# Query and key columns inside the value products of a four-layer graph network, with a different order of the softmax and of the layers around it

## The chip, the cores and the metric

The kernel runs on one core of one Trainium2 chip. The metric is the device time of one execution in microseconds (us), median of several runs. A profiled execution gives the times of single instructions; its span is close to, but not the same as, the timed runs.

Engines are named as in the profile: PE (TensorE, matmul) with PEld (its weight loads), DVE (VectorE), ACT (ScalarE), POOL (GpSimd) and SP (SyncE, which here issues the DMAs). Matmuls write to PSUM, from which DVE and ACT read.

## The reference

128 graphs of 128 nodes with 512 features, and one weighted adjacency matrix each, go through four layers. Each layer's output is added to its input and normalized over the features. All data is float32.

```python
def reference(x, adj, ...):
    # layer 0: normalized adjacency (with self loops), times x, times a weight
    #   Ah = A + I;  dh = rsqrt(sum(Ah));  An = dh Ah dh;  out = relu(An x W0 + b0)
    x = layernorm(x + L0(x, adj))
    # layer 1: attention-like weights, one number per node
    #   q, k = split(x Wqk^T)  (64 columns each);  v = x Wv^T
    #   w = sum over m of (q k^T / 8) * adj;   w = softmax over the nodes;  out = w * v
    x = layernorm(x + L1(x, adj))
    # layer 2: mean over neighbours, joined with x
    #   agg = (A x) / deg;  out = relu([x, agg] W2^T)
    x = layernorm(x + L2(x, adj))
    # layer 3: like layer 0 without relu:  out = An (x W3 + b3)
    x = layernorm(x + L3(x, adj))
```

## The kernel before

**Tiling.** The graphs are taken in groups of four (`G = 4`, 32 groups, index `t`). One group's x is a tile of 128 partitions (nodes) by 4 x 512.

**Block products.** Each 512 x 512 weight is split into 2 x 2 blocks of 256, and a product of activations and weight is made of seven block products instead of eight (a Strassen-Winograd form), named B11, T1, B21, T2, B22, T3, T4 in `project` (L517). The activations are split the same way, over pairs of graphs (`q`), the two graphs of a pair (`r`) and the halves of the features (`h`). `left_sums` (L495) forms four sums of activation blocks on POOL (each 128 x 512 for a group), `weight_sums` (L373) the ones of the weights, once. One block product is four matmuls of 256 columns, each of which the profile shows as two instructions. The results meet in a few PSUM banks (`ps_b`, five of them); DVE and ACT read them out between the products into blocks `s`, `u2`, `u5`. `fin` adds a finished block to x; `norm_stats` (L613) and `norm_last` (L592) normalize rows.

**Layer 1.** `l1_turn` (L669) gives x transposed; `l1_qk` (L678) makes queries and keys by 16 matmuls of 128 columns per group into `p_qk`; ACT copies them out (`kd`, `qs`). `l1_scores` (L697) multiplies the adjacency by the keys (`p_sc`, 65 columns: 64 keys and one column that yields row sums `rs` for layer 3's bias) and reduces on DVE to one number `w` per node. `l1_softmax` (L717) turns `w` on PE (`p_w`) and forms the softmax `e`; `l1_weights` (L732) turns it back (`p_ws`) to `ws`. `l1_out` (L739) is the product of the values, where `fin` adds block times `ws` to x; parts that come before `ws` is known wait in a list.

**Aggregates.** `aggregate` (L458) multiplies x by an adjacency on PE into `p_agg` (`ps_t`, three banks), ACT copies it out. The adjacency of group t+1 is loaded, scaled and transposed in `prep` (L854: `load`, `prep_rows`, `prep_turn`); two hops through DRAM and DVE transposes do the turn. `turn_x` (L467) does the same with x for layers 1 and 2 (`xT1`, `xT2`): SP issues the copies to DRAM and back, DVE transposes 32 x 32 blocks.

**Order.** Every instruction is first recorded. PE's order is the one written out by hand in the loop below; `hooks` insert work behind a block product, and `tails` postpone the last product (T4) of a projection into the next one. A planner (`Plan.schedule`) then orders the other engines by due times which it derives from estimated durations. DVE, ACT, POOL and SP run their queues in that order.

The loop over groups works on group t in layers 0 and 1 and on group u = t-1 in layers 2 and 3:

```python
        if t > 1:
            l0_out(t, {B21: [lambda: l2_agg(u, 1)]})
            prep(t + 1)
            tails.append(lambda: l1_turn(t))
        l2_out(u, {T3: [lambda: l1_qk(t, 0)]} if t > 1 else {...})
        if t < last:
            l0_agg(t + 1)
        finish_tails()
        if t > 1:
            l1_qk(t, 1)
        l1_out(t, {B11: [lambda: l1_scores(t)], B21: [lambda: l1_softmax(t)], T3: [lambda: l3_agg(u)]})
        l3_bias(u)
        l3_out(u)
        if t < last:
            l2_turn(t)
            l2_agg(t, 0)
```

In the profile every instruction has the line of the planner's `emit` (L270), so groups are told apart by tile names.

Of the kernel before, what the change touches and what calls it, by code (L numbers as in the profile page):

```python
# [15 lines left out]
P = 128  # L16
# [6 lines left out]
ATT = 64  # L23
LN_EPS = 1e-5
# [286 lines left out]
def kernel(  # L311
# [32 lines left out]
    def load(t):  # L344
        if t == 1:
            a = tp.tile([P, 2, G, P], FP, tag="y", name="adj_1", bufs=3)[:, 0]
        else:
            a = ap.tile([P, G, P], FP, tag="adj", name=f"adj_{t}", bufs=1)
        nc.sync.dma_start(a, adj[t * G:(t + 1) * G].rearrange("g n m -> n g m"))
        xi = xp.tile([P, G, F], FP, tag="x", name=f"x_{t}")  # L350
        for g in range(0, G, 2 if t == 0 else G):
            k = slice(g, g + (2 if t == 0 else G))
            nc.sync.dma_start(xi[:, k], x[t * G:(t + 1) * G][k].rearrange("g n f -> n g f"))
        st["adj", t], st["x", t] = a, xi
# [38 lines left out]
    wqk_sb = const.tile([P, C, 2 * ATT], FP, tag="wqk_sb", name="wqk_sb")  # L393
    for b in range(Q):
        nc.sync.dma_start(wqk_sb[b * K:(b + 1) * K], wqkT.rearrange("(b c k) m -> b k c m", b=Q, c=C)[b])
    wv_sb = weight(wvT, "wv_sb", nc.sync, turned=True)
# [9 lines left out]
    def prep_rows(t):  # L406
        a = st["adj", t]
        deg = sp.tile([P, G], FP, tag="deg", name=f"deg_{t}")
        nc.vector.tensor_reduce(deg, a, AX.X, ALU.add)
        dh = sp.tile([P, G], FP, tag="dh", name=f"dh_{t}")  # L410
        nc.vector.tensor_scalar(dh, deg, 1.0, None, ALU.add)
        d = sp.tile([P, G], FP, tag="d", name=f"d_{t}")
        nc.gpsimd.tensor_tensor(d, dh, nhalf, ALU.pow)
        dm = sp.tile([P, G], FP, tag="dm", name=f"dm_{t}")
        nc.vector.tensor_scalar(dm, deg, DEG_EPS, None, ALU.max)
        rdeg = sp.tile([P, G], FP, tag="rdeg", name=f"rdeg_{t}")
        nc.vector.reciprocal(rdeg, dm)
        ana = tp.tile([P, 2, G, P], FP, tag="y", name=f"ana_{t}", bufs=3)
        nc.vector.tensor_tensor(ana[:, 0], a, ident[:, None, :].to_broadcast([P, G, P]), ALU.add)
        nc.vector.tensor_tensor(ana[:, 0], ana[:, 0], per_graph(d), ALU.mult)  # L420
        nc.vector.tensor_tensor(ana[:, 1], a, per_graph(rdeg), ALU.mult)
        st["ana", t], st["d", t], st["dm", t] = ana, d, dm
# [72 lines left out]
    def left_sums(name, t, eng=nc.gpsimd, pairs=(slice(0, 2),)):  # L495

        a = st[name, t].rearrange("p (q r) (h c) n -> p q r h c n", r=2, h=2)
        s = [tp.tile([P, 2, 2, P], FP, tag=f"s{i}", name=f"{name}s{i}_{t}", bufs=3) for i in (1, 2, 3, 4)]
        for q in pairs:
            a11, a12, a21, a22 = a[:, q, 0, 0], a[:, q, 0, 1], a[:, q, 1, 0], a[:, q, 1, 1]  # L500
            s1, s2, s3, s4 = (v[:, q] for v in s)
            eng.tensor_tensor(s1, a21, a22, ALU.add)
            eng.tensor_tensor(s2, s1, a11, ALU.subtract)
            eng.tensor_tensor(s3, a11, a21, ALU.subtract)
            eng.tensor_tensor(s4, a12, s2, ALU.subtract)
        st[name, t] = {B11: a[:, :, 0, 0], B21: a[:, :, 0, 1], B22: s[3], T4: a[:, :, 1, 1], T1: s[0], T2: s[1], T3: s[2]}
# [10 lines left out]
    def project(name, t, parts, first, c11, fin, hooks=None, after=lambda: None, early=True,  # L517
                when=lambda f: f(), pairs=(0, 1)):
# [26 lines left out]
        def block(tag):  # L545
            return tp.tile([P, 2, H], FP, tag=tag, name=f"{tag}_{name}_{t}", bufs=1 if tag in ("u5", "sb") else 2)[:, qs]
# [5 lines left out]
        if early:  # L552
            product(g, B21, False)
            when(lambda: c11(g, block))
# [4 lines left out]
        if not early:  # L559
            product(g, B21, False)  # L560
            when(lambda: c11(g, block))
# [6 lines left out]
        when(lambda: (fin(0, 1, u2), norm_stats(name, t, 0, pairs)))  # L568
# [100 lines left out]
    def l1_turn(t, turn=turn_x, rows=(0, 1)):  # L669
        if rows[0] == 0:  # L670
            left("xT1", t)
        for r in rows:
            turn("xT1", t, r)
        st["x1T", t] = st["xT1", t]
        if rows[-1] == 1:
            left_sums("xT1", t)

    def l1_qk(t, r):  # L678

        xT = st["x1T", t]  # L680
        if r == 0:
            st["p_qk", t] = ps_t.tile([P, G, 2 * ATT], FP, tag="pt", name=f"p_qk_{t}")
        p = st["p_qk", t]
        with nc.unit():
            for g in (r, 2 + r):
                for c in range(C):
                    nc.tensor.matmul(p[:, g, :], xT[:, g, c, :], wqk_sb[:, c, :], start=(c == 0), stop=(c == C - 1))
        if r == 0:
            return
        kd = tp.tile([P, G, ATT + 1], FP, tag="kd", name=f"kd_{t}", bufs=1)  # L690
        nc.scalar.copy(kd[:, :, 0:ATT], p[:, :, ATT:2 * ATT])
        nc.scalar.copy(kd[:, :, ATT], st["d", t])
        qs = tp.tile([P, G, ATT], FP, tag="qs", name=f"qs_{t}", bufs=1)
        nc.scalar.mul(qs, p[:, :, 0:ATT], 1.0 / ATT ** 0.5)
        st["qk", t] = qs, kd

    def l1_scores(t):  # L697


        qs, kd = st.pop(("qk", t))  # L700
        d, dm = st["d", t], st["dm", t]
        p = ps_t.tile([P, G, ATT + 1], FP, tag="pt", name=f"p_sc_{t}")
        with nc.unit():
            for g in range(G):
                nc.tensor.matmul(p[:, g, :], st["arT", t][:, g, :], kd[:, g, :], start=True, stop=True)
        w = sp.tile([P, G], FP, tag="w", name=f"w_{t}")
        scr = tp.tile([P, F], FP, tag="row", name=f"scr_{t}", bufs=1)[:, 0:G * ATT].rearrange("p (g a) -> p g a", g=G)
        nc.vector.tensor_tensor(scr, p[:, :, 0:ATT], qs, ALU.mult)
        nc.vector.tensor_reduce(w, scr, AX.X, ALU.add)
        nc.vector.tensor_tensor(w, w, dm, ALU.mult)  # L710
        rs = sp.tile([P, G], FP, tag="rs", name=f"rs_{t}")
        nc.vector.tensor_tensor(rs, p[:, :, ATT], dm, ALU.mult)
        nc.vector.tensor_tensor(rs, rs, d, ALU.add)
        nc.vector.tensor_tensor(rs, rs, d, ALU.mult)
        st["w", t], st["rs", t] = w, rs
# [16 lines left out]
    def l1_weights(t):  # L732
# [4 lines left out]
        st["ws", t] = ws  # L737

    def l1_out(t, hooks=None):  # L739
        z = st["x", t]  # L740

        def fin(r, h, blk):
            for q in range(2):
                g = 2 * q + r
                zg = z[:, g, h * H:(h + 1) * H]
                nc.vector.scalar_tensor_tensor(zg, blk[:, q, :], st["ws", t][:, g:g + 1], zg, ALU.mult, ALU.add)

        def when(f):
            if ("ws", t) in st:
                f()  # L750
            else:
                pending.append(f)

        def weights():
            l1_weights(t)
            for f in pending:
                f()

        pending = []
        hooks[T3] = [weights] + hooks[T3]  # L760
        project("v", t, [("xT1", wv_sb)], copy_first, lambda p, b: fin(0, 0, p), fin, hooks,
                early=False, when=when)
# [34 lines left out]
    def l3_agg(t):  # L797
        left("agg3", t)
        for g in (0, 2, 1, 3):
            aggregate("agg3", t, g, st["anT", t])  # L800
# [14 lines left out]
    def l3_out(t, left="agg3", pairs=(0, 1)):  # L815
        def fin(r, h, blk):
# [3 lines left out]
        project("o3", t, [(left, w3_sb)], copy_first, lambda p, b: fin(0, 0, p), fin,  # L820
                after=lambda: store(t), pairs=pairs)
# [9 lines left out]
    def begin():  # L831
# [7 lines left out]
        weight_sums(wv_sb, nc.vector)  # L839
        l0_out(1)  # L840
        l1_turn(0, turn_on_tensor, (0,))
        finish_tails()
        l1_qk(0, 0)
        l1_turn(0, turn_on_tensor, (1,))
        l1_qk(0, 1)
        for w in (w2x_sb, w2a_sb, w3_sb):
            weight_sums(w, nc.gpsimd)
        l1_out(0, {B11: [lambda: l1_scores(0)], B21: [lambda: l1_softmax(0)],
                   T3: [lambda: l1_turn(1, turn_on_tensor), lambda: l1_qk(1, 0)]})
        finish_tails()  # L850
        l1_qk(1, 1)
        l2_both(0, 0)

# [7 lines left out]
    for t in range(1, NT):  # L861
        u = t - 1
        if t > 1:
            l0_out(t, {B21: [lambda: l2_agg(u, 1)]})
            prep(t + 1)
            tails.append(lambda: l1_turn(t))
        l2_out(u, {T3: [lambda: l1_qk(t, 0)]} if t > 1 else {B21: [lambda: l2_both(0, 1), lambda: prep(2)]})
        if t < last:
            l0_agg(t + 1)
        finish_tails()  # L870
        if t > 1:
            l1_qk(t, 1)
        l1_out(t, {B11: [lambda: l1_scores(t)], B21: [lambda: l1_softmax(t)], T3: [lambda: l3_agg(u)]})
        l3_bias(u)
        l3_out(u)
        if t < last:
            l2_turn(t)
            l2_agg(t, 0)
# [5 lines left out]
    for q in range(2):  # L884
        l3_agg_pair(last, q, nc.gpsimd)
        l3_bias(last, (2 * q, 2 * q + 1))
        l3_out(last, f"agg3{q}", (q,))
# [33 lines left out]
```

## Time and profile before

| what | value |
|---|---|
| timed runs (3) | 2481.28 us median, 2480.01 to 2484.1 |
| profiled span | 2479.5 us, granted PE clock 0.998 |
| PE busy | 2458.4 us |
| DVE busy | 1813.6 us |
| POOL busy | 1336.5 us |
| ACT busy | 976.6 us |
| DMA | 241.24 MB in all, 97 GB/s mean |

A group of the profile is a set of like instructions: engine, operation, output tile and inputs, shape, count, busy time and mean length. The timeline of an engine gives start and length of its instructions in us from the span's start; an arrow in brackets names the idle time before one and what ended it. Since matmuls overlap in PE's pipeline, what one costs is read from the distance between starts.

### The profile page before, as it was taken

How to read it: one execution, taken by the hardware profiler on the slowest of the kernel's cores; microseconds unless marked ns; L12 is line 12 of the kernel's file. 1: busy time of each engine (PE TensorE's matmuls, PEld its weight loads, DVE VectorE, ACT ScalarE, POOL GpSimd, SP SyncE). 2: the span in 40 equal slices, each digit the busy share in tenths (PEclk: the TensorE clock that was granted, in tenths of full speed). 3: DMA queues.
4: the chain of work that ended last, by engine and by line, in shares of the span. 5: the costliest groups of instructions: out<-in, count | busy, mean ns of one | idle time of the engine just before them, and what ended most of it. 6: DMA issues, size and time to landing. Idle time of an engine off the chain costs nothing.

```text
span 2479.5 us, 37052 instructions
## 1 busy us (share of the span) xinstructions
PE 2458.4 (99%) x13486; PEld 2206.8 (89%) x13486; DVE 1813.6 (73%) x3165; ACT 976.6 (39%) x1989; POOL 1336.5 (54%) x1522
## 2 busy tenths in 40 slices
PE   8999999999999999999999999999999999999998
PEld 7898998989989889889899998998998999989987
DVE  7677777777777777777777777777777777777665
ACT  3334334443334344344433343433434334443335
POOL 6455555646455555555555564645555555655443
PEclk9999999999999999999999999999999999999999
DMA  5142434423434324344333343343442434433220
GB/s 178 35 111 74 106 93 113 121 82 88 108 97 124 100 75 115 89 116 112 81 97 102 103 124 94 77 107 93 124 111 69 110 90 115 118 80 88 77 60 34
DMA packets 392629, 241.24 MB, mean 97 GB/s; under 512 B 140288, under 2 KB 356864, under 8 KB 392448
## 3 DMA queue, kind: packets, MB, share of 16 engines
q1 hardware_dynamic: 392448, 238.88, 36.1%
q8 instruction: 107, 1.75, 0.3%
q14 instruction: 74, 0.61, 0.1%
HBM read 126.62 MB, written 112.20 MB: 96 GB/s over the span
## 4 chain that ended last, share of the span: by engine, by line
PE 98%; DMA 1%; ACT 0%; DVE 0%; SPq 0%; POOL 0%; issue 0%; ACTq 0%; POOLq 0%; DVEq 0%
PE p_o L270 62%; PE p_v L270 16%; PE p_agg L270 14%; PE p_qk L270 5%; PE p_sc L270 1%; DMA x<-in_x_dram 0%; SPq L270 0%; DVE x L270 0%; PE p_ws L270 0%; DMA w2x_sb<-in_L_gnn_W_dram 0%; PE p_w L270 0%; ACT xT L270 0%; PE p_xT L270 0%; POOL last L270 0%; ACT agg L270 0%
## 5 line engine op out<-in xcount | busy, mean ns | idle before, releaser
L270 ACT COPY agg<-p_agg 128x512 f32<-128x512 f32 x384 | 221.0, 583 | 578.6 <-PE p_agg L270 578.6
L270 PE MATMUL p_o<-w_sb,agg 128*128 128x256 f32 x1536 | 353.5, 379 | 1.2 <-ACT s_o L270 0.7
L270 PEld LDWEIGHTS p_o<-w_sb,agg 128*128 128x128 f32 x1536 | 286.6, 190 | 38.3 <-ACT s_o L270 1.1
L270 PE MATMUL p_o<-w2x_sb,xT2s 128*128 128x256 f32 x1024 | 263.0, 379 | 1.5 <-DVE xT2s L270 1.5
L270 PE MATMUL p_o<-w2a_sb,agg2s 128*128 128x256 f32 x1024 | 262.8, 379 | 0.0
L270 POOL TENSOR_TENSOR xT1s<-xT 128x512 f32<-128x512 f32 x64 | 94.3, 1473 | 286.7 <-DVE xT L270 228.8
L270 PE MATMUL p_agg<-anT,x 128*128 128x128 f32 x2048 | 243.9, 277 | 0.2 <-DVE anT L270 0.2
L270 PEld LDWEIGHTS p_agg<-anT,x 128*128 128x128 f32 x2048 | 235.5, 192 | 1.2 <-DVE anT L270 0.4
L270 PE MATMUL p_v<-wv_sb,xT1s 128*128 128x256 f32 x1024 | 233.3, 381 | 0.0
L270 PE MATMUL p_o<-w_sb,agg0s 128*128 128x256 f32 x1024 | 229.5, 382 | 3.5 <-DVE u_o L270 2.6
L270 POOL TENSOR_TENSOR agg3s<-agg 128x512 f32<-128x512 f32 x62 | 84.1, 1356 | 270.9 <-ACT agg L270 270.9
L270 PEld LDWEIGHTS p_o<-w_sb,agg0s 128*128 128x128 f32 x1024 | 192.6, 191 | 30.7 <-DVE u_o L270 3.0
L270 PEld LDWEIGHTS p_o<-w2x_sb,xT2s 128*128 128x128 f32 x1024 | 194.4, 190 | 28.3 <-DVE xT2s L270 2.0
L270 PE MATMUL p_o<-w_sb,agg3s 128*128 128x256 f32 x992 | 219.2, 379 | 0.0
L270 PEld LDWEIGHTS p_o<-w2a_sb,agg2s 128*128 128x128 f32 x1024 | 194.6, 190 | 26.5
L270 PEld LDWEIGHTS p_v<-wv_sb,xT1s 128*128 128x128 f32 x1024 | 189.6, 190 | 27.3
L270 PEld LDWEIGHTS p_o<-w_sb,agg3s 128*128 128x128 f32 x992 | 188.5, 190 | 25.6
L270 ACT ACTIVATE x<-x,nmro,rstdo 128x512 f32<-128x512 f32 x257 | 198.8, 809 | 4.3
L270 PE MATMUL p_o<-w2x_sb,xT 128*128 128x256 f32 x768 | 197.6, 380 | 1.8 <-ACT s_o L270 1.1
L270 PE MATMUL p_o<-w2a_sb,agg 128*128 128x256 f32 x768 | 197.1, 379 | 0.0
L270 DVE TENSOR_TENSOR u_o<-p_o,s_o 128x512 f32<-128x512 f32 (+1 forms) x132 | 89.2, 675 | 146.1 <-PE p_o L270 146.1
L270 PE MATMUL p_v<-wv_sb,xT 128*128 128x256 f32 x768 | 182.0, 380 | 1.9 <-DVE u_v L270 1.9
(141 smaller groups left out, 4674.8 us busy)
## 6 DMA issues: line engine op xcount, KB each, us to landing
x<-in_x_dram SPq DMA_DIRECT2D x31, 1024.0 KB, 5.1
out_dram<-x SPq DMA_DIRECT2D x31, 1024.0 KB, 5.4
xT2s<-x SPq DMA_DIRECT2D x120, 256.0 KB, 2.6
xT2y<-xT2s SPq DMA_DIRECT2D x240, 128.0 KB, 2.9
xT1s<-x SPq DMA_DIRECT2D x120, 256.0 KB, 2.5
xT1y<-xT1s SPq DMA_DIRECT2D x240, 128.0 KB, 3.3
sa<-ana SPq DMA_DIRECT2D x120, 128.0 KB, 3.4
ya<-sa SPq DMA_DIRECT2D x120, 128.0 KB, 3.2
```

Source lines behind the costliest of these rows:

```text
L270: getattr(getattr(self.nc, op.engine), method)(*[v.real() if isinstance(v, Ref) else v for v in args], **{k: v.real() if isinstance(v, Ref ...
```

## The change

- `l1_qk` goes. Queries and keys are 64 more columns of each weight block of the values (`V = H + ATT = 320`): the left column block gets the queries, the right one the keys, and the seven block products of `l1_out` compute them too. The result stays in SBUF in four tiles `v00` to `v11`; each pair q of a region has a PSUM bank of its own.
- Scores come behind the whole product of the values and layer 3's aggregates; `l1_softmax` is a hook of the first block product of `l3_out`, and `l1_add` (turn of the softmax, addition of `ws` times v to x, statistics) a hook of its third. `l3_out` takes B21 behind T1 (`early` false) except in the last group.
- Both halves of layer 2's aggregates move into the next `l0_out` (hooks B21 and T1); one half stood ahead of it before.
- The adjacency is loaded straight into the tile `ana` (tag `y`, three buffers) and scaled in place; the single buffer `adj` goes. The third sum of `left_sums` overwrites a block of its operand, so one of four tags of sums goes; `u2` has one buffer instead of two.
- The order of the first groups is written out anew: both `l1_out` products come before layer 2 of group 0, and the loop starts at t = 2.

```diff
-    wqk_sb = const.tile([P, C, 2 * ATT], FP, tag="wqk_sb", name="wqk_sb")
+    wqk_sb = tp.tile([P, C, 2 * ATT], FP, tag="row", name="wqk_sb", bufs=1)
 ...
-    wv_sb = weight(wvT, "wv_sb", nc.sync, turned=True)
+    wv_sb = const.tile([P, 2, 7, V], FP, tag="wv_sb", name="wv_sb")
+    for h in range(2):
+        for j in range(2):
+            for b in range(Q):
+                nc.sync.dma_start(wv_sb[b * K:(b + 1) * K, :, 2 * h + j, 0:H], ...)
+            nc.scalar.copy(wv_sb[:, :, 2 * h + j, H:V], wqk_sb[:, 2 * h:2 * h + 2, j * ATT:(j + 1) * ATT])
 ...
-            eng.tensor_tensor(s3, a11, a21, ALU.subtract)
+            eng.tensor_tensor(a21, a11, a21, ALU.subtract)
 ...
     def l1_scores(t):
-                nc.tensor.matmul(p[:, g, :], st["arT", t][:, g, :], kd[:, g, :], start=True, stop=True)
+                nc.tensor.matmul(p[:, g, :], st["arT", t][:, g, :], st["v", t][g % 2, 1][:, g // 2, H:V + 1],
+                                 start=True, stop=True)
-        nc.vector.tensor_tensor(scr, p[:, :, 0:ATT], qs, ALU.mult)
+        for r in range(2):
+            nc.vector.tensor_tensor(scr...[:, :, r], p...[:, :, r, 0:ATT], st["v", t][r, 0][:, :, H:V], ALU.mult)
         nc.vector.tensor_reduce(w, scr, AX.X, ALU.add)
-        nc.vector.tensor_tensor(w, w, dm, ALU.mult)
+        nc.vector.scalar_tensor_tensor(w, w, 1.0 / ATT ** 0.5, dm, ALU.mult, ALU.mult)
 ...
+    def l1_out(t, hooks):
+        def product(p, k, fresh, then):
+            for q in range(2):
+                with nc.unit():
+                    for c in range(2):
+                        nc.tensor.matmul(p[q], a[k][:, q, c, :], wv_sb[:, c, k, :], ...)
+                then(p[q], q)
+            for f in hooks.get(k, ()):
+                f()
+        def add(to, other):
+            return lambda p, q: nc.vector.tensor_tensor(to[:, q, 0:V], p, other[:, q, 0:V], ALU.add)
+        g = region()
+        product(g, B11, True, lambda p, q: nc.scalar.copy(s[:, q, 0:V], p))
+        finish_tails()
+        q5 = region()
+        product(q5, T1, True, add(out[1, 1], s))
+        product(g, B21, False, lambda p, q: nc.scalar.copy(out[0, 0][:, q, 0:V], p))
+        v = region()
+        product(v, T2, True, add(out[0, 1], s))
+        product(q5, B22, False, add(out[0, 1], out[0, 1]))
+        product(v, T3, False, add(out[1, 1], out[1, 1]))
+        product(v, T4, False, add(s, s))
+    def l1_add(t):
+        nc.tensor.transpose(p[:, :G], st.pop(("e", t)), ident[:G, :G])
+        nc.vector.tensor_copy(ws, p[:, :G])
+        for r in range(2):
+            for g in (r, 2 + r):
+                for h in range(2):
+                    nc.vector.scalar_tensor_tensor(zg, st["v", t][r, h][:, g // 2, 0:H], ws[:, g:g + 1], zg,
+                                                   ALU.mult, ALU.add)
+            norm_stats("v", t, r, (0, 1))
 ...
     def l3_agg(t):
-        for g in (0, 2, 1, 3):
+        for g in (0, 1, 3, 2):
 ...
     def begin():
+        l1_out(0, {T3: [lambda: l1_turn(1, turn_on_tensor)]})
+        l1_out(1, {B11: [lambda: l1_scores(0)], T1: [lambda: l1_softmax(0)], B21: [lambda: l1_add(0)]})
         l2_both(0, 0)
+        l2_out(0, {B21: [lambda: l2_both(0, 1), lambda: prep(2)], T2: [lambda: l1_scores(1)],
+                   B22: [lambda: l1_softmax(1)], T3: [lambda: l1_add(1)]})
+        l0_agg(2)
+        l2_turn(1)
+        l0_out(2, {B21: [lambda: l2_agg(1, 0)], T1: [lambda: l2_agg(1, 1)]})
+        l3_agg(0)
+        l3_bias(0)
+        l3_out(0)
 ...
-    for t in range(1, NT):
+    for t in range(2, NT):
         u = t - 1
+        if t > 2:
+            l0_out(t, {B21: [lambda: l2_agg(u, 0)], T1: [lambda: l2_agg(u, 1)]})
+        tails.append(lambda: l1_turn(t))
+        prep(t + 1)
+        l2_out(u)
         if t < last:
             l0_agg(t + 1)
-        l1_out(t, {B11: [lambda: l1_scores(t)], B21: [lambda: l1_softmax(t)], T3: [lambda: l3_agg(u)]})
+        l1_out(t, {})
+        l3_agg(u)
+        l1_scores(t)
         l3_bias(u)
-        l3_out(u)
+        l3_out(u, {B11: [lambda: l1_softmax(t)], B21: [lambda: l1_add(t)]})
         if t < last:
             l2_turn(t)
-            l2_agg(t, 0)
```

## The prediction

> **What bounds the kernel now.** I read the page first: busy time, then the chain that ended last.
>
> ```profile
> PE 2458.4 (99%) x13486; PEld 2206.8 (89%) x13486; DVE 1813.6 (73%) x3165; ACT 976.6 (39%) x1989; POOL 1336.5 (54%) x1522
> ...
> PE 98%; DMA 1%; ACT 0%; DVE 0%; SPq 0%; POOL 0%; issue 0%; ACTq 0%; POOLq 0%; DVEq 0%
> ```
>
> TensorE (PE) holds 98% of the chain. The list of PE's waits adds up to some 13 us, all near the start and the end; one period, from one block product of layer 2 to the same one of the next group, is 76.13 us (1045.66 to 1121.79) without a wait. So a PE instruction saved is time saved, and a PE wait added is time added. Next, PE in order of time in one group (start, length, instructions):
>
> ```profile
> 1016.11 1.95 PE L270 MATMUL p_qk<-wqk_sb,xT 128*128 128x128 f32 x16
> 1017.90 3.78 PE L270 MATMUL p_agg<-anT,x 128*128 128x128 f32 x32
> ...
> 1026.76 1.89 PE L270 MATMUL p_v<-wv_sb,xT 128*128 128x256 f32 x8
> 1028.49 1.00 PE L270 MATMUL p_sc<-kd,arT 128*128 128x65 f32 x8
> 1029.33 1.94 PE L270 MATMUL p_v<-wv_sb,xT1s 128*128 128x256 f32 x8
> 1031.11 1.89 PE L270 MATMUL p_v<-wv_sb,xT 128*128 128x256 f32 x8
> 1032.83 0.27 PE L270 MATMUL p_w<-ident,w 128*4 128x128 f32 x1
> ```
>
> Prices are differences of starts: sixteen instructions of 128 columns take 1.79 us (112 ns each), eight of 256 take 1.73 (216 ns), the eight of the scores 0.84. Two block products (3.5 us) lie between the scores and `p_w`, which turns their row sums `w`; until `p_ws` at 1038.22, which turns the softmax, three more (5.2 us). VectorE (DVE) and GpSimd (POOL) meanwhile:
>
> ```profile
> 1029.60 0.42 DVE L270 TENSOR_TENSOR scr<-p_sc,qs 128x256 f32<-128x256 f32 x1 [1.29 <-PE p_sc L270]
> 1030.05 0.42 DVE L270 TENSOR_REDUCE w<-scr 128x4 f32<-128x256 f32 x1
> 1030.51 1.24 DVE L270 TENSOR_TENSOR w<-w,dm 128x4 f32<-128x4 f32 x1
> ...
> 1033.60 0.27 DVE L270 TENSOR_REDUCE mx<-p_w 4x1 f32<-4x128 f32 x1
> ...
> 1034.56 0.15 DVE L270 RECIPROCAL rsum<-ssum 4x1 f32<-4x1 f32 x1 [0.43 <-ACT e L270]
> ```
>
> ```profile
> 1030.46 1.27 POOL L270 TENSOR_TENSOR agg0s<-agg 128x512 f32<-128x512 f32 x1
> ```
>
> Four numbers per partition took 1.24 us: `w` ended when POOL's sum ended. Before, 3.5 us of PE work covered this.
>
> **What the Trainium skill says.** "SBUF — State Buffer", on the shared port pair: an exclusive lock between DVE and POOL; a DVE instruction with two SBUF inputs and a POOL instruction exclude each other, and the first to start has it to its end. The trace agrees (`w` above). "TensorE: Matmul & The Clock Gate", on the issue gap: N/2.4 + 2.5 ns, 109 ns at 256 columns; fp32 here takes 216, so the trace's prices are used; its straight line in N holds.
>
> **The change part by part.** Sums are against the profiled span, 2479.5 us; the timed runs' median is 1.8 us higher.
>
> 1. *Columns.* The 28 products of the values (56 instructions) go from 256 to 320 columns. Not shown before; the line through 112 and 216 ns gives 268, two cycles per column at 2.4 GHz give 269. So 56 x 53 = +2.98 us, less the 32 of `p_qk`, 3.58 us: -0.60 us a group (ends -0.67 and -0.59), -19.2 us in 32 groups.
> 2. *Evacuation.* Ten adds of 320 and four ACT copies replace five adds of 512 (0.69 each) and a copy; `kd` and `qs` go. 320 is estimated at 0.16 + 1.04 ns x 320 = 0.49 us. DVE gains about 2 us in 76, with 25% idle. The narrow place is the last product but one, followed by the last into the same bank: each half lasts 4 x 0.269 = 1.08 us, the add needs 0.2 + 0.49. Nothing, unless DVE is held: 0 to 0.3 us a group; I take 0.
> 3. *Softmax behind.* In the changed program's order PE runs four layer-3 aggregates, the scores, one block product (1.73 us), `p_w`, two products (3.45), `p_ws`. Count from S, the end of the scores' issue. The aggregates end 0.90 us apart; copies and POOL follow as at 1038 to 1043, so POOL's first sum starts at S-0.86 and runs to 0.41, the second 0.49 to 1.76, the third 1.84 to 3.11, the fourth from 3.07 (it waits for nothing of the third). DVE: three of the four biases of layer 3 are done by S-0.9 (their graphs' aggregates are read by then, POOL idle); product in two halves and reduce from 0.27 to 1.23 (0.27 from the end of the issue to `scr`, as at 1029.60); `w`, with two SBUF inputs, from 1.26, held until 1.78. PE wants `w` at 1.73: with 0.05 us of signal and a lost weight prefetch (0.1) it loses 0.2 us a group.
> 4. *What queues behind `w`.* `rs` from PSUM, `rs` times `d` (held until 3.13), a bias of layer 3 on 512 elements (`x<-b_sb,rs,x`), then `mx`: `p_ws` and all of PE wait for that bias. It comes free just as POOL's fourth sum wants the ports. If the bias goes first it ends at 3.66; `mx` 3.6, another small `rs` held until POOL's fourth sum ends at 4.9, the reciprocal behind it, `e` done 5.3 (0.16 + 0.27 later). `p_ws` is due at 1.73 + 0.11 + 3.45 + 0.2 = 5.5: no wait. If POOL goes first, the bias ends at 4.9 and `e` at 6.2 (1.4 us after the start of `mx`: 0.96 to the reciprocal as at 1033.60 to 1034.56, then 0.43): PE loses 1.07 us in all, not 0.2.
>
> Which it is, the trace shows in one place of the same form, a held small instruction with another right behind it:
>
> ```profile
> 38.24 1.26 DVE L270 TENSOR_SCALAR dh<-deg 128x4 f32<-128x4 f32 x1
> 39.42 0.16 DVE L270 TENSOR_SCALAR dm<-deg 128x4 f32<-128x4 f32 x1
> ```
>
> ```profile
> 38.22 1.26 POOL L270 TENSOR_TENSOR agg0s<-agg,agg0s 128x512 f32<-128x512 f32 x1
> 39.44 1.26 POOL L270 TENSOR_TENSOR agg0s<-agg 128x512 f32<-128x512 f32 x1
> ```
>
> `dm` started 0.02 us before POOL's next sum and was not held. Two long instructions in a row do alternate with POOL: additions to `ana` at 1020.15 and 1021.89 took 1.71 and 1.65, not 0.68. The bias behind a small `rs` resembles the first; I take it, with doubt.
>
> 5. *Aggregates of layer 2 in layer 0; adjacency in a `y` buffer; T3 in place; fewer buffers.* From `p_ws` to these aggregates lie six products (10.5 us); what they need: `ws` 0.5, four additions 0.4 each (three took 1.28), one product's add 0.6, statistics 1.5 (1.28 + 0.30), POOL 1.3 (1029.21 to 1030.51), ACT 1.8 (0.20 + 1.52): 7.3, and ACT's part stands behind the copy of layer 0's first product, which ends 7.9 us after `p_ws`, so 9.7. SP issues the second half of x, normalized 12.4 us after `p_ws` (the copy's 7.9, a bias sum of POOL 1.3, POOL 1.3, ACT 1.8, each row as above), ahead of the second hop of the first; from there to the transposes took 5.1 us before (1055.5 to 1060.61), then 1.3 of DVE: 19.3, where layer 2 starts 21.0 us after `p_ws`. Before, this margin was 8 us. The adjacency load starts later, but some 15 us lie between turn and use. T3 in place is the same POOL instruction to another tile. All 0, hidden by these products, with up to 1 us a group at risk.
> 6. *First groups.* `p_qk`'s waits (1.95 us at 71.41, then a slow clock) go; scores and softmax of group 0 now have one product each to hide behind. The weights' DMAs are 16 of half the size instead of 8, and layer 2's weights are wanted later. 0, within 4 us.
> 7. *End.* Before, 15.9 us lie between the last `p_ws` (2404.88) and the aggregates (2420.79); now three products, 5.2 us, against the 7.3 of step 5 (2.1 us of wait); the transposes of x then stand behind two copies of 0.56 (1.1), and the second half of the graphs has some 0.3 left to wait: +3.5 us (2 to 6).
>
> Sum: 2479.5 - 19.2 + 30 x 0.2 + 3.5 = 2469.8; as a timed run 2472 us. Its own range: 2464 to 2478.
>
> **Rivals.**
> - *POOL first* (ends slower): one mechanism at one place, the bias ahead of `mx` in DVE's queue. 2479.5 - 19.2 + 30 x 1.07 + 3.5 = 2495.9, as a run 2498. It decides against the change from 0.52 us of PE wait a group on ((19.2 - 3.5)/30). For it: long instructions alternate. Against: `dm`.
> - *All waits hidden*: 2479.5 - 19.2 + 3.5, as a run 2466. Against: `w` cannot end before POOL's second sum.
> - *Other new waits*: the turn of x for layer 2 or item 2 cost 1 us a group and more, and waits add up past 2 us, behind which PE ran slower before (at 73.62 sixteen 128-column matmuls took 3.05 us, not 1.79): over 2505. Against: the margins of 5.
>
> **How the numbers follow.** Chances: forecast 0.5, POOL first 0.32, all hidden 0.1, others 0.08. Since both signs have weight, the range goes from the hidden case less 3 us, 2463, to POOL first plus 4, 2502; outside lie the last rival and edges. About 0.2% (5 us) is what a measurement tells from no change. Faster: 0.5 and 0.1 less 0.03 of the forecast's edge, 0.57; slower: 0.32 + 0.08 less 0.03, 0.37; same 0.06.
>
> **What would show it.** `p_v` at 269 ns a matmul and no `p_qk`: step 1. A PE wait of 0.1 us at each `p_w`, and none at `p_ws`: steps 3 and 4; about 1 us at `p_ws`, with DVE's bias lasting over 1.2 us, is the first rival. Waits of `p_agg` or `p_o` on `x` or `xT` in mid-run, or of `p_v` on DVE, would show step 5 or 2 wrong. A period over 76.13 us makes the forecast wrong whatever start and end do.

## The result, and the profile after

The changed kernel takes 2489.61 us (median of six runs, 2487.8 to 2490.23); the kernel before, measured beside it, takes 2481.15 (2480.01 to 2484.1). The ratio is 1.0032, 95% interval 1.0019 to 1.0045: slower by 8 us, where the forecast was faster by 9. The profiled span is 2487.9 us against 2479.5.

First the page of the changed kernel, its line of busy times and the shares of the chain that ended last:

```profile
PE 2443.3 (98%) x12462; PEld 2087.7 (84%) x12462; DVE 1792.9 (72%) x3357; ACT 990.7 (40%) x2057; POOL 1302.7 (52%) x1522
...
PE 90%; DVE 7%; ACT 1%; issue 1%; DMA 1%; SPq 0%; POOL 0%; ACTq 0%; POOLq 0%; DVEq 0%
```

TensorE is busy 15 us less than before, so the saving is there. But VectorE, which held nothing of the chain, now holds 7% of it. The list of TensorE's waits (total us, number, longest) says where the two meet:

```profile
PE p_ws L271 <- DVE e L271: 22.3, 31, 0.7
```

One wait of 0.7 us in each of the 30 groups of the loop (and one more near the start), at the turn of the softmax; before, no wait in mid-run was listed. Next one group in order of time, TensorE first (start, length, instructions, idle time before and its releaser):

```profile
1038.80 3.73 PE L271 MATMUL p_agg<-anT,x 128*128 128x128 f32 x32
1042.37 1.00 PE L271 MATMUL p_sc<-v,arT 128*128 128x65 f32 x8
1043.21 1.95 PE L271 MATMUL p_o<-w_sb,agg 128*128 128x256 f32 x8
1045.15 0.27 PE L271 MATMUL p_w<-ident,w 128*4 128x128 f32 x1
1045.25 1.89 PE L271 MATMUL p_o<-w_sb,agg3s 128*128 128x256 f32 x8
1046.98 1.89 PE L271 MATMUL p_o<-w_sb,agg 128*128 128x256 f32 x8
1049.59 0.19 PE L271 MATMUL p_ws<-ident,e 4*128 4x4 f32 x1 [0.72 <-DVE e L271]
```

S, the end of the scores' issue, is 1043.21. A block product, eight instructions of the profile, takes 1.73 us without a wait; `p_w` comes 1.94 us after S, so 0.21 us are lost ahead of it. Two block products take 3.46 us; from 1045.25 to `p_ws` there are 4.34, so 0.88 us are lost there. Of these, 0.09 are no wait: the last instruction ahead of `p_ws` takes that much longer in the kernel before too, where nothing waits. VectorE and GpSimd in the same stretch:

```profile
1043.41 0.49 DVE L271 TENSOR_TENSOR scr<-p_sc,v 128x128 f32<-128x128 f32 x2 [0.91 <-PE p_sc L271]
1043.93 0.42 DVE L271 TENSOR_REDUCE w<-scr 128x4 f32<-128x256 f32 x1
1044.39 0.61 DVE L271 SCALAR_TENSOR_TENSOR w<-w,dm 128x4 f32<-128x4 f32 x1
1044.92 0.15 DVE L271 TENSOR_TENSOR rs<-p_sc,dm 128x4 f32<-128x4 f32 x1
1045.11 1.24 DVE L271 TENSOR_TENSOR rs<-rs,d 128x4 f32<-128x4 f32 x1
1046.27 1.83 DVE L271 SCALAR_TENSOR_TENSOR x<-b_sb,rs,x 128x512 f32<-128x512 f32 x1
1048.02 0.27 DVE L271 TENSOR_REDUCE mx<-p_w 4x1 f32<-4x128 f32 x1
...
1049.17 0.27 DVE L271 TENSOR_SCALAR e<-e,rsum 4x128 f32<-4x128 f32 x1
```

```profile
1042.34 1.29 POOL L271 TENSOR_TENSOR agg3s<-agg 128x512 f32<-128x512 f32 x1 [7.12 <-ACT agg L271]
1043.71 1.27 POOL L271 TENSOR_TENSOR agg3s<-agg3s,agg 128x512 f32<-128x512 f32 x1
1045.06 1.27 POOL L271 TENSOR_TENSOR agg3s<-agg,agg3s 128x512 f32<-128x512 f32 x1
1046.28 1.27 POOL L271 TENSOR_TENSOR agg<-agg 128x512 f32<-128x512 f32 x1
```

The bias `x<-b_sb,rs,x` lasts 1.83 us where the same instruction elsewhere takes 0.75: it stood still until GpSimd's last sum ended. `mx`, behind it in the queue, starts at S+4.81 although `p_w` has been there since S+1.94, and `e` is ready at S+6.23. The bias' record starts 10 ns ahead of the sum's here, and 8 to 21 ns ahead in all 30 groups; GpSimd went first in all 30.

The period from one `p_w` to the next is 76.40 us against 76.13. Over the 29 groups from the second layer 2 to the last but one that is 8.8 us, 0.9 of it from a few groups with 0.15 to 0.35 us more. The start gave 2.4 us (the second group's layer 2 begins at 153.9 instead of 156.3), and what follows the last but one layer 2 took 2.0 more: -2.4 + 8.8 + 2.0 = 8.4 us, the difference of the spans.

### The profile page after: what moved, and what is told of

Same layout as the page of the kernel before. It is cut to its first block, busy times and chain, and to the rows that moved or that the text cites. A ratio compares the mean times of both kernels' runs of the same rounds, so it can differ in the third digit from the quotient of the medians.

```text
span 2487.9 us, 35407 instructions
## 1 busy us (share of the span) xinstructions
PE 2443.3 (98%) x12462; PEld 2087.7 (84%) x12462; DVE 1792.9 (72%) x3357; ACT 990.7 (40%) x2057; POOL 1302.7 (52%) x1522
## 4 chain that ended last, share of the span: by engine, by line
PE 90%; DVE 7%; ACT 1%; issue 1%; DMA 1%; SPq 0%; POOL 0%; ACTq 0%; POOLq 0%; DVEq 0%
PE p_o L271 55%; PE p_v L271 19%; PE p_agg L271 14%; DVE x L271 2%; DVE rs L271 2%; DVE w L271 1%; PE p_sc L271 1%; DVE scr L271 1%; ACT e L271 1%; DMA x<-in_x_dram 0%; SPq L271 0%; DVE e L271 0%; DVE mx L271 0%; PE p_ws L271 0%; DVE rsum L271 0%
## 5 line engine op out<-in xcount | busy, mean ns | idle before, releaser
L271 PE MATMUL p_o<-w_sb,agg 128*128 128x256 f32 x2048 | 471.5, 380 | 1.7 <-DVE u_o L271 1.0
L271 PEld LDWEIGHTS p_o<-w_sb,agg 128*128 128x128 f32 x2048 | 385.9, 190 | 54.0 <-ACT s_o L271 1.1
L271 PE MATMUL p_v<-wv_sb,xT 128*128 128x320 f32 x1024 | 291.4, 432 | 0.0
L271 DVE TENSOR_TENSOR v<-p_v,v 128x320 f32<-128x320 f32 x316 | 154.7, 490 | 173.2 <-PE p_v L271 172.1
L271 PE MATMUL p_o<-w2x_sb,xT 128*128 128x256 f32 x1024 | 263.3, 379 | 1.7 <-ACT s_o L271 1.1
L271 PEld LDWEIGHTS p_v<-wv_sb,xT 128*128 128x128 f32 x1024 | 192.1, 190 | 75.9
L271 PEld LDWEIGHTS p_o<-w2x_sb,xT 128*128 128x128 f32 x1024 | 194.1, 190 | 32.6 <-ACT s_o L271 1.9
L271 PE MATMUL p_v<-wv_sb,xT1s 128*128 128x320 f32 x768 | 217.4, 433 | 0.1
L271 PEld LDWEIGHTS p_o<-w2a_sb,agg 128*128 128x128 f32 x1024 | 194.6, 190 | 26.4
L271 DVE TENSOR_TENSOR u_o<-p_o,u_o 128x512 f32<-128x512 f32 (+1 forms) x196 | 131.1, 670 | 118.4 <-PE p_o L271 118.2
```

What stands on the lines that cost most here:

```text
L271: getattr(getattr(self.nc, op.engine), method)(*[v.real() if isinstance(v, Ref) else v for v in args], **{k: v.real() if isinstance(v, Ref ...
```

## The experiments

Theory A is the prediction's first rival, made exact: the bias ahead of `mx` is held by GpSimd's last sum, and carries `mx`, `e` and `p_ws` with it. Theory B says that the chain from the scores to `e` is too long for the products left, bias or not. Theory C says that the loss comes from the wider products or the moved aggregates. Each kernel below is the changed kernel with the edit shown, unless it says otherwise. "Period" is the usual distance from one `p_w` to the next; before 76.13, changed 76.40. The first four runs, the next four and the last three were measured at different times; the kernel before, measured beside them, took 2481.0, 2482.5 and 2481.2 us, so runs of different sets are better compared by ratio and period.

| run | us, median | ratio to before, 95% | period |
|---|---|---|---|
| bias behind the softmax | 2482.60 | 1.0006 (0.9997-1.0015) | 76.20 |
| scores first | 2487.79 | 1.0026 (1.0015-1.0036) | 76.40 |
| no last sum | 2465.93 | 0.9937 (0.9923-0.9952) | 75.63 |
| bias directly behind `w` | 2474.49 | 0.9972 (0.9963-0.9982) | 75.96 |
| bias behind, identity held back | 2474.23 | 0.9967 (0.9955-0.9979) | 75.87 |
| scores first, identity held back | 2472.04 | 0.9958 (0.9945-0.9972) | 75.82 |
| pause ahead of the last sum | 2470.11 | 0.9949 (0.9936-0.9963) | 75.79 |
| before, aggregates moved | 2482.48 | 0.9999 (0.9991-1.0007) | 76.13 |
| scores first and bias behind | 2463.50 | 0.9927 (0.9913-0.9942) | 75.57 |
| bias without its scalar | 2466.27 | 0.9941 (0.9925-0.9958) | 75.63 |
| bias at `w`, identity held back | 2466.44 | 0.9941 (0.9926-0.9956) | 75.63 |

**The bias behind the softmax**

```diff
+    def bias_behind(u):
+        e_scaled = nc.ops[-1]
+        l3_bias(u, (2,))
+        nc.ops[-1].preds.add(e_scaled)
 ...
-        l3_bias(u)
-        l3_out(u, {B11: [lambda: l1_softmax(t)], B21: [lambda: l1_add(t)]})
+        l3_bias(u, (0, 1, 3))
+        l3_out(u, {B11: [lambda: l1_softmax(t), lambda: bias_behind(u)], B21: [lambda: l1_add(t)]})
```

> The changed kernel with one instruction moved: the bias of the last graph of layer 3 comes on VectorE behind the scaling of e instead of ahead of mx; everything is still computed. Theory A (the bias is held by GpSimd's last sum and carries mx, e and p_ws with it): mx goes at S+3.1, where S is the end of the issue of the scores, right after the second rs; e is scaled at about S+4.5 instead of S+6.24, p_ws, due at about S+5.5, waits for nothing, and 30 groups get 0.8 to 0.9 us back: 2489.6 - 26 = 2463 us (2460 to 2466); the 0.2 us before p_w stay. Theory B (the chain behind the scores is too long for the 24 products in any case): p_ws still waits 0.3 us or more, and the time is above 2475. Theory C (the wait is only where the time shows; it is lost in the wider value products or in the moved aggregates): 2487 to 2491.

Measured: 2482.6 us, a miss of every theory: better than the changed kernel, but 20 us short of A. VectorE's timeline shows why:

```profile
1038.97 1.76 DVE L271 TENSOR_TENSOR ana<-ana,ident 128x512 f32<-128x512 f32 x1
1040.65 0.47 DVE L271 TENSOR_TENSOR scr<-p_sc,v 128x128 f32<-128x128 f32 x2
...
1041.98 2.46 DVE L271 TENSOR_TENSOR rs<-rs,d 128x4 f32<-128x4 f32 x2
1044.36 0.27 DVE L271 TENSOR_REDUCE mx<-p_w 4x1 f32<-4x128 f32 x1
```

The planner, free to place what it likes, had put another instruction of two SBUF inputs into the gap, the addition of the identity to a later group's adjacency. The changed kernel runs it in layer 0's time, where it takes 0.68 us. Here it stands ahead of `scr`, GpSimd's first sum holds it (1.76 us, 0.68 when free), and the whole chain starts 0.7 us later. So this kernel moved two things, not one.

**The scores ahead of layer 3's aggregates**

```diff
-        l3_agg(u)
         l1_scores(t)
+        l3_agg(u)
```

> The changed kernel with the eight score products recorded ahead of the 32 aggregate products of layer 3 instead of behind them, so that 3.6 us more of TensorE's work stand between the scores and p_w; everything is still computed. Theory A and theory B both: VectorE's chain still meets GpSimd's sums, but p_w and p_ws wait for nothing: 0.2 and 0.9 us of 30 groups come back and their restarts with them, 2489.6 - 34 = 2455 us (2452 to 2459), which is below the kernel before. Theory C: 2487 to 2491, the loss being elsewhere. A result between 2459 and 2475 would mean that the sums of layer 3, now started 0.7 us later, bring a wait of their own at the third term of the projection.

Measured: 2487.79 us, no better than the changed kernel within 2 us; A's number was off by 33. The wait ahead of `p_w` is gone, the one at `p_ws` is not. VectorE between `p_w` (1044.73) and `mx`:

```profile
1044.32 1.77 DVE L271 SCALAR_TENSOR_TENSOR x<-b_sb,rs,x 128x512 f32<-128x512 f32 x1
1046.01 1.75 DVE L271 TENSOR_TENSOR ana<-ana,ident 128x512 f32<-128x512 f32 x1
1047.68 0.27 DVE L271 TENSOR_REDUCE mx<-p_w 4x1 f32<-4x128 f32 x1
```

Again the identity has moved, now between the bias and `mx`, and both are held by GpSimd's sums. The number spoke for C; the trace says that the mechanism of A acted twice.

**No last sum**

```diff
-            eng.tensor_tensor(a21, a11, a21, ALU.subtract)
+            if name != "agg3":
+                eng.tensor_tensor(a21, a11, a21, ALU.subtract)
```

> The changed kernel without GpSimd's fourth sum of layer 3's aggregates, the one in place (agg<-agg): it leaves out that subtraction, so the third term of layer 3's projection uses the block as it was. VectorE's order is that of the changed kernel: the bias stands ahead of mx. Theory A: nothing holds the bias behind the third sum, it runs from S+3.13 to about S+3.7, e is scaled at about S+5.1, before p_ws is due at S+5.5, and the time is about 2463 us (2460 to 2467), as with the bias moved. Theory B: an unheld bias is still too much in this place, p_ws waits 0.3 us or more, above 2475. Theory C: 2487 to 2491.

Measured: 2465.93 us, inside A's range. VectorE's order is the changed kernel's, and the bias, in its old place, runs free:

```profile
1039.40 0.74 DVE L271 SCALAR_TENSOR_TENSOR x<-b_sb,rs,x 128x512 f32<-128x512 f32 x1
```

S is 1036.35 in this group; `e` is ready at S+5.2, and no wait of `p_ws` in mid-run is left. B falls: with the bias still ahead of `mx`, the products cover the chain. C falls as the main cause: with columns and aggregates as they are, the kernel is 15 us faster than before.

**The bias directly behind `w`**

```diff
-        l1_scores(t)
-        l3_bias(u)
+        l1_scores(t, lambda: l3_bias(u, (2,)))
+        l3_bias(u, (0, 1, 3))
```

`l1_scores` calls what it is handed directly behind its last instruction on `w`, and `rs` and `mx` are ordered behind that bias.

> The changed kernel with the last bias of layer 3 moved on VectorE to directly behind w, and ahead of mx and of both rs; everything is still computed. It meets GpSimd's sums one earlier: the bias is free to start at about S+1.8, within some tens of ns of the third sum, which follows the second by 0.08 us. Theory A1 (whoever's record starts first takes the lock): bias from S+1.8 to 2.4, the third sum after it, mx at 2.5, e by S+4.1. Theory A2 (GpSimd, which queued behind the same release, goes first): the bias is held until the third sum ends at S+3.1 and lasts 1.8 us by its record, mx at 3.7, e by S+5.1. In both p_ws waits for nothing, and the time is 2463 us (2459 to 2467); the trace tells which of A1 and A2. Theory B: above 2475. Theory C: 2487 to 2491.

Measured: 2474.49 us, above A's range. One line of VectorE and one of GpSimd answer A1 or A2:

```profile
1040.46 0.74 DVE L271 SCALAR_TENSOR_TENSOR x<-b_sb,rs,x 128x512 f32<-128x512 f32 x1
```

```profile
1040.59 1.73 POOL L271 TENSOR_TENSOR agg3s<-agg,agg3s 128x512 f32<-128x512 f32 x1
```

A1: the bias led by 132 to 138 ns in the 30 groups, went first in all, and GpSimd's sum was the one that waited (1.73 us instead of 1.27). `p_ws` waits for nothing, but `p_w` is now listed with a wait of 0.31 us for `w`: once more the identity stood ahead of `scr`.

Where a run below is said to hold the identity back, and in the run with a pause, that addition comes behind the scaling of `e`. The three lines that do it are the same in each:

```diff
         nc.vector.tensor_tensor(ana[:, 0], a, ident[:, None, :].to_broadcast([P, G, P]), ALU.add)
+        if t > 3:
+            nc.ops[-1].preds.add(st.pop(("scaled", t - 2)))
 ...
         nc.vector.tensor_scalar(e, e, rsum, None, ALU.mult)
+        st["scaled", t] = nc.ops[-1]
```

**The bias behind the softmax, identity held back**

> The run before with the bias behind the softmax again, and the addition of the identity to a later group's adjacency (ana<-ana,ident) held back behind the scaling of e, where the changed kernel has it too; in that earlier run it had come ahead of the scores' products with the values, was held by GpSimd's first sum for 1.1 us and delayed w to S+2.05. VectorE's order is now w, rs, rs, rs, mx. Theory A, with first come first served: the second rs is held to S+3.1, the third follows it at once, mx at S+3.3, e at S+4.7, p_ws does not wait: 2489.6 - 26 = 2463 us (2460 to 2466). Theory A with the rule that whoever waits at the release goes before the next instruction of the engine that just held the lock: the third rs, four elements wide, is held by GpSimd's last sum to S+4.4, e at S+5.7, p_ws waits some 0.25 us instead of 0.9: 2489.6 - 19 = 2470 us (2467 to 2473). Theory C (the loss is elsewhere): 2482 to 2491.

Measured: 2474.23 us, 8 us better than without those lines and 1 us above the range of A's second form; the period is 75.87. The two `rs`, and the last sum:

```profile
1040.06 2.47 DVE L271 TENSOR_TENSOR rs<-rs,d 128x4 f32<-128x4 f32 x2
```

```profile
1041.24 1.26 POOL L271 TENSOR_TENSOR agg<-agg 128x512 f32<-128x512 f32 x1
```

The third `rs` was held by the last sum, and `p_ws` waits 0.19 us. But it needs no rule about who waits at a release: that `rs` has to wait for the one before it, and its record starts 90 to 104 ns after the sum's. First come, first served is enough to explain it. Taking the bias away was thus not enough, because four numbers per partition are held as long as 512.

**The scores first, identity held back**

> The scores ahead of layer 3's aggregates again, with the same addition of the identity held back behind the scaling of e; in the earlier run it stood between the last bias and mx and was held 1.1 us, so that mx went 3.0 us behind p_w. Theory A: the bias is still held by GpSimd's sums, to 1.3 us behind p_w, mx goes there, e is scaled some 2.4 us behind p_w, 1.1 us ahead of the moment at which p_ws is due (3.5 us behind p_w), and neither p_w nor p_ws waits: 2489.6 - 34 = 2455 us (2452 to 2459). Theory C: 2484 to 2491.

Measured: 2472.04 us, 16 us better than with the identity in the gap, and still 17 above A. `mx` now goes where A had it, 1.28 us behind `p_w`; what came after it was not expected:

```profile
1041.77 1.36 DVE L271 TENSOR_SCALAR e<-e,rsum 4x128 f32<-4x128 f32 x1
```

```profile
1041.78 1.26 POOL L271 TENSOR_TENSOR agg<-agg 128x512 f32<-128x512 f32 x1
```

The scaling of `e` itself was held (1.36 us, 0.27 when free), in all 30 groups, with a record that starts 12 to 23 ns ahead of the sum's. It has only one tensor input. The Trainium skill, "VectorE: DVE Perf Modes", section "What auto-detection actually checks", has a single-source instruction from SBUF to SBUF enter a mode of two ports when the outermost sizes of source and destination are both even or equal, and "SBUF — State Buffer", section "Who interferes with whom", counts `tensor_scalar` among the operations that can take the shared pair in this way. The trace agrees: 1.36 us beside the sum.

**A pause on GpSimd ahead of the last sum**

```diff
+            if name == "agg3":
+                nc.gpsimd.tensor_scalar(a21[:, 0, 0, 0:2], a21[:, 0, 0, 0:2], 1.0, None, ALU.mult)
             eng.tensor_tensor(a21, a11, a21, ALU.subtract)
```

> The changed kernel with one instruction more on GpSimd, a multiplication of two elements by 1.0 between the third and the last sum of layer 3's aggregates (an instruction of that width, rstdv, takes 0.36 us in the trace after), and the addition of the identity held where the changed kernel has it; everything is still computed, and VectorE's order is the changed kernel's, the bias ahead of mx. The last sum can now start only some 0.3 us behind the release of the third. Theory A: the bias takes the lock in that gap, ends at S+3.8 to S+4.2, e is scaled at S+5.1 to S+5.5, p_ws waits for at most 0.1 us, and the last sum ends about 0.9 us later than before, which nothing waits for: 2463 us (2460 to 2468). If GpSimd goes first all the same, e comes at S+6.6 and the time is 2498 to 2502. Theory C: 2487 to 2491.

Measured: 2470.11 us. An instruction more, and 19 us less than the changed kernel:

```profile
1039.68 0.74 DVE L271 SCALAR_TENSOR_TENSOR x<-b_sb,rs,x 128x512 f32<-128x512 f32 x1
```

```profile
1039.82 0.68 POOL L271 TENSOR_SCALAR agg<-agg 128x2 f32<-128x2 f32 x1
1040.59 1.27 POOL L271 TENSOR_TENSOR agg<-agg 128x512 f32<-128x512 f32 x1
```

The bias, 143 to 145 ns ahead in the 30 groups, took the lock, and GpSimd's pause stood behind it (0.68 us). The number is 2 us above the range because the later last sum now holds the third `rs`, and `e` comes at S+5.6.

**The kernel before with the aggregates moved**

```diff
-            l0_out(t, {B21: [lambda: l2_agg(u, 1)]})
+            l0_out(t, {B21: [lambda: l2_agg(u, 0)], T1: [lambda: l2_agg(u, 1)]})
 ...
             l2_turn(t)
-            l2_agg(t, 0)
```

> The kernel before with one part of the change alone: both halves of layer 2's aggregates are issued within the next layer 0, one product earlier each, and none at the end of the loop. The prediction's step 5 has this at nothing: 2481 us (2478 to 2484), period 76.13 us. If the aggregates are where the changed kernel loses, 2486 to 2492; if they are what makes its aggregate blocks 0.1 us shorter, 2475 to 2478.

Measured: 2482.48 us beside 2482.51 of the kernel before, period 76.13. In the kernel before, this part of the change costs nothing and gives nothing.

**Both cures at once**: scores first, bias behind the scaling of `e`, identity held back.

> Both cures at once: the scores ahead of layer 3's aggregates, the last bias behind the scaling of e, and the addition of the identity held behind it too; everything is still computed. Worked out from the run with the scores first, where mx still stood behind the bias: mx can go 0.15 us behind p_w, e is scaled by about 2.3 us behind p_w even if GpSimd's third sum holds it, and p_ws is due 3.5 us behind p_w. Theory A (every loss sits in the two waits): period 76.40 - 0.21 - 0.88 + 0.12 = 75.43 us, 0.97 us a group less than the changed kernel: 2489.6 - 29 = 2460.5 us (2458 to 2464), with no wait for p_w or p_ws. Theory B or C (something else in the changed kernel costs time too): 2466 or more.

Measured: 2463.5 us, inside A's range and 0.9927 of the kernel before: the best of these kernels, and faster than the kernel before and the changed one. TensorE's own rows:

```profile
1035.17 0.27 PE L271 MATMUL p_w<-ident,w 128*4 128x128 f32 x1
1035.28 1.89 PE L271 MATMUL p_o<-w_sb,agg3s 128*128 128x256 f32 x8
1037.01 1.89 PE L271 MATMUL p_o<-w_sb,agg 128*128 128x256 f32 x8
1038.83 0.22 PE L271 MATMUL p_ws<-ident,e 4*128 4x4 f32 x1
```

From 1035.28 to `p_ws` there are 3.55 us, 0.09 over the two block products, without a wait. The period is 75.57, not 75.43: single slow steps of 0.05 to 0.1 us where TensorE changes from one kind of product to another remain, as in the kernel before, and closing the gap ahead of `p_w` was worth 0.06 us net (75.63 with the last sum left out, 75.57 here), not 0.21. So the 2455 us forecast for the scores first counted more than the two waits hold: without either wait the kernel takes 2463.5.

**The bias without its scalar**

```diff
-            nc.vector.scalar_tensor_tensor(z[:, g, :], b3_sb, st["rs", t][:, g:g + 1], z[:, g, :],
+            nc.vector.scalar_tensor_tensor(z[:, g, :], b3_sb, 1.0 if g == 2 else st["rs", t][:, g:g + 1], z[:, g, :],
```

> The changed kernel with the third graph's bias multiplied by the constant 1.0 instead of by a column of rs: it leaves out that scaling by the row sums. Order and width are the changed kernel's; only the read of the scalar is gone. If reading its scalar from SBUF makes the bias late at the lock, it now goes ahead of GpSimd's last sum: e at S+5.0, and 2466 to 2471 us. If not (the engine as such comes later to the lock than its recorded start says): the bias is still held 1.8 us although its record starts 8 to 21 ns ahead of the sum's, and 2488 to 2491 us.

Measured: 2466.27 us, the first of the two outcomes:

```profile
1037.61 0.68 DVE L271 SCALAR_TENSOR_TENSOR x<-b_sb,x 128x512 f32<-128x512 f32 x1
```

```profile
1037.63 1.78 POOL L271 TENSOR_TENSOR agg<-agg 128x512 f32<-128x512 f32 x1
```

The order is the same and the lead is the same, 8 to 22 ns. With the scalar read from SBUF, GpSimd went first in 30 of 30 groups; with a constant, VectorE did in 30 of 30, and the last sum waited 0.5 us. The bias also gets shorter, 0.68 us instead of 0.74 to 0.75, as if the read of the scalar came in front of the rest; that it does is not shown.

**The bias at `w`, identity held back**

> The last bias directly behind w again, with the addition of the identity held back behind the scaling of e as the changed kernel has it: in the earlier run it came ahead of the scores' products, was held by the first sum, and cost p_w 0.31 us. Theory A: w at S+1.8 as in the changed kernel, p_w loses 0.2 us as there, the bias starts more than 100 ns ahead of the third sum or is held by it to S+3.1, e comes by S+5.3 in either case, and p_ws waits for nothing: period 75.63 us as with the last sum left out, 2489.6 - 23 = 2466.5 us (2463 to 2470). Theory C: 2474, no change from the earlier run.

Measured: 2466.44 us, period 75.63, as A had it. So the identity was what kept the earlier run from A's number.

## Why the prediction was wrong, step by step

- **What bounds the kernel**: right. The periods above follow from TensorE's rows plus its gaps.
- **Step 1, columns**: right. An instruction of 320 columns takes 269 ns; 56 x 53 ns less 3.57 us is the -0.60 us a group.
- **Step 2, evacuation**: right in what it decides: no wait of `p_v` for VectorE is listed in mid-run. VectorE did not gain work on balance, though: its busy time fell from 1813.6 to 1792.9 us, since other instructions are held for less (`anT<-anT,d` takes 0.69 us in the mean, 1.67 before).
- **Step 3, up to `w`**: right. The sums of GpSimd start at S-0.87, 0.50, 1.85 and 3.07 (predicted S-0.86, 0.49, 1.84 and 3.07), and `p_w` loses 0.21 us (0.2). Net it counts for less, 0.06 us by the run with both cures.
- **Step 4, the order of bias and last sum**: this step failed. "If the bias goes first" was taken; GpSimd went first in every group. `e` came at S+6.23, the rival's 6.2, and `p_ws` lost 0.88 us. The analogy failed at a point that can be named: the `dm` that slipped in ahead of GpSimd took no scalar from SBUF, and the bias does. That taking the scalar away turns the order is shown by the run without it; by what means the scalar makes the bias late is not. With the constant the period is 75.63; the forecast's 0.4 us under 76.13 would be 75.73.
- **Step 5, aggregates**: right. The aggregates' part is shown by the kernel before with that part alone; the other parts were not run alone, but no wait of `p_agg` or of layer 2's `p_o` is listed in mid-run. One sum of this step is wrong: 12.4 + 5.1 + 1.3 is 18.8, not 19.3, which leaves more margin.
- **Steps 6 and 7**: the start gave 2.4 us, of which two groups of columns are 1.2, so the rest of step 6 is -1.2 (0 within 4). The end cost 2.0 us, of which 0.3 are what every group loses (76.40 less 76.13); the rest, 1.7, lies just under step 7's range (3.5, from 2 to 6).
- **The rival "POOL first"** had the mechanism, and was 8 us too high (2498). Its 1.07 us a group of losses were all counted as new. Some of it was in the kernel before already: there, too, the last instruction ahead of `p_ws` took 0.31 us (0.22 elsewhere), and the eight behind the scores 1.78 us from start to start (1.73 elsewhere). With these and smaller differences of the same kind the net was +0.27 us a group, not +0.47, 6 us in 30 groups. The end, 1.8 us shorter than forecast, and the start, 1.2 us better, account for the rest.

Where did the 19 us of step 1 go? They stayed, on TensorE, and were paid back at one place, `p_ws`: leaving out the last sum gave 0.77 us a group back (76.40 less 75.63), 23 us in 30 groups. The change placed a chain that needs the ports beside the four sums of GpSimd that need them too; before, only `w` met a sum, and there was one block product more ahead of `p_w` and one more ahead of `p_ws` to hide it.

## What to carry to other kernels

When a chain of short VectorE instructions runs beside long GpSimd instructions, list every VectorE instruction in it that takes both ports, small ones and single-input SBUF-to-SBUF ones like the scaling of `e` too, and give each the whole GpSimd instruction as its price unless it leads clearly. An analogy for who goes first must match the form of the instruction, the scalar operand included. After any reordering, look at what the planner moved into the gap before believing the time: here an unrelated addition cost three experiments 8, 16 and 8 us.

## What the runs showed of the hardware

- A recorded start does not decide who gets the shared ports to within some 20 ns. Beside a sum of 128 x 512, instructions with a scalar read from SBUF lost with leads of 8 to 23 ns (the bias in 30 groups, the scaling of `e` in 30) and won with 132 to 138 (the bias directly behind `w`, 30). One place between these stands near the start of the changed kernel and of each kernel made from it (11 traces): `x<-v,ws,x`, which reads its scalar from SBUF too, led the sum `agg0s<-agg` by 93 to 99 ns and went first in all (the sum took 1.51 us instead of 1.27). The bias with a constant won with 8 to 22 (30). So, worked out from these leads, VectorE's claim with such a scalar comes between 23 and 93 ns later than its record says, measured against GpSimd's, and without one less than 8 ns later. The difference in length, some 0.07 us, would fit; that it is the cause is not shown.
- Of GpSimd's sums in a row, one that needs the result of the one before starts 1.35 us after that one's start, an independent one 1.22, before the end of the one before. In the gap of 0.08 us the bias with its scalar from SBUF got ahead of the third sum; ahead of the last one it got only with a constant. The two-element pause needs no result of the third sum and still started 1.35 us after it, so dependence is not the only thing that makes such a gap.
- A held instruction stands until the sum has ended, whether it has 4 or 512 elements per partition: `rs` 1.24 us in all, the bias 1.28 us until the end of the sum and 0.55 more.
- A long record of GpSimd is not in itself a long hold. Its power on two elements per partition, `rstdv<-rstdv,nhalf`, takes 0.71 us; `x<-u_o,x`, with two SBUF inputs of 512, started 0.05 to 0.64 us behind it in 30 places of the changed kernel, inside its record, and took 0.68 us, as when free.
